# Columns whose layer-1 products are done at once: their transposed adjacency goes from SBUF into the weight table, not by way of DRAM

## The chip, the core and the metric

The kernel runs on one core of one Trainium2 chip. The metric is the device time of one execution in microseconds (us). Engines are named as the profile names them: PE multiplies matrices and transposes, DVE and ACT work on vectors, POOL issues the indirect gathers, SP issues plain DMAs; ACT issues some DMAs too. All DMAs run on the same sixteen DMA engines. A profile is one execution seen by the hardware profiler.

## What is computed

Two layers over a graph of 3,327 nodes (padded to 3,328 = 26 x 128) with 128 features and a sparse weighted adjacency matrix `adj`, symmetric in its pattern, about 2% full. Layer 0 is graph attention with four heads, layer 1 a normalised graph convolution:

```python
h = jnp.maximum(_layernorm(x, axis=-1), 0.0)
# for each of 4 heads
x1 = h @ w1
x2 = h @ w2
E = leaky_relu(x1[:, None, :] + x2[None, :, :], 0.01)
s = tanh(E @ a / 8.0) * 8.0
s = jnp.exp(s) * adj
s = s / jnp.sum(s, axis=-1, keepdims=True)
out = leaky_relu(s @ h @ Wlin.T, 0.01)
x = x + jnp.concatenate(heads, axis=-1) @ w

h = jnp.maximum(_layernorm(x, axis=-1), 0.0)
A_t = adj + jnp.eye(n)
D_inv = A_t.sum(axis=1) ** (-0.5)
A_norm = D_inv[:, None] * A_t * D_inv[None, :]
x = x + relu(A_norm @ (h @ W.T + b))
```

## The kernel before

Rows are handled in 26 blocks of 128. A row has few neighbours, so layer 0 does not form the full score matrix. `prep(b)` finds, for each row of block b, its neighbours' numbers; `gather` fetches one table row per neighbour with indirect DMAs (`DMA_INDIRECT`, L605, 128 table rows at a time, issued by POOL); the scores and the weighted sums are then made from what was fetched.

**The tables.** There are two tables in DRAM, `tables[0]` and `tables[1]`; block b uses `tables[b % 2]`. A table has one row of 776 numbers for each node: 64 numbers of adjacency (`FEAT`), 648 of features and products (`BODY`), 64 more of adjacency (`FEAT`). The 648 are written once, at the start. The adjacency numbers belong to a block: row n holds the weights `adj[r, n]` of block b's 128 rows r, the first 64 on one side of `BODY` and the other 64 on the other side, so that a gathered row brings its weights with it. They are the transposed 128 rows of `adj`, and are renewed for each block.

**How the weights get there.** `prep(b)` holds block b's rows of `adj` in SBUF (`adjb`, 128 x 3328, one buffer). `tables_step(j0)` (from L370) takes four column blocks (512 columns): PE transposes them into a PSUM bank (L373), ACT copies the bank to `at` in SBUF (L375; three buffers), and ACT issues a DMA that writes `at` to a scratch in DRAM, `AT_d` (L378). For 3,328 columns there are seven steps, the last of two column blocks. When all are done, `k.turned` is set, and `weights(b)` may be issued by SP: one DMA (L615) copies the whole 1,664 KB from `AT_d` into the table, DRAM to DRAM, in pieces of 512 bytes (the last 64 numbers of one row and the first 64 of the next lie side by side); a second, tiny one (L617) writes the first row's first 64 numbers.

**Who else reads `at` and `AT_d`.** Layer 1 needs the same transposed adjacency, times the finished features of the nodes in those columns. For columns whose features are already finished when block b is prepared, the product is made at once: `finished(b)` = max(0, 4 (b // 4) - 2) column blocks. `known_step` multiplies `at` with `x_sb` (PE, L387) and adds to `part1` (L391, L393), which goes to DRAM when complete (L395). The other columns are read back from `AT_d` late, at the end of layer 0 and in layer 1 (L929, L946).

**Order of the work.** All instructions are laid out in one order written by generators; each engine runs its own in that order. `prep` is a generator of up to 72 steps a block, advanced by `advance` in `slot()` alongside the groups of attention work of the block before; it runs about one to one and a half blocks ahead. Its course: steps of `codes` (L418) and of MAX8 on 64 segments (L430), with a `tables_step` at every eighth segment; then `turned`; then ACT's pass over `adjb` that sums the rows (`deg`, L451, 2.96 us), which is the last reader of `adjb`; then SP's load of the next block's rows into it (L359, 1,664 KB); then eight rounds of `select(r)` (L461, L464), the index lists, and the extras. POOL's gathers stand in a queue: 64 for the lists and 4 for the extras (`ge`) a block; `weights(b + 1)` stands in that queue behind the second group of gathers of block b, and is held until block b + 1 is turned. Gathered rows have four buffers `g` of eight gathers each; a buffer is free when PE has made the products `ag` (L680) from it.

**After layer 0's blocks** come the strips of layer 1 (L929 on), which read what is left from `AT_d`.

Of the kernel before, what the change touches and what calls it, by code (L numbers as in the profile page):

```python
# [10 lines left out]
AF = mybir.ActivationFunctionType  # L11
# [4 lines left out]
P = 128  # L16
# [48 lines left out]
FEAT = 64  # L65
BODY = 648
ROW = FEAT + BODY + FEAT
# [164 lines left out]
def _sparse_layers(tc, nc, x, adj, w1, w2, a, wlin, w, gw, gb, gb_sb, gwT, x_sb, dinv, flag, ident, out):  # L232
# [13 lines left out]
    NP, D = x.shape  # L246
    H = w1.shape[0]
    NB = NP // P
# [5 lines left out]
    NW = NT // WT  # L254
    LATE = 1

    with ExitStack() as l0:
        res = l0.enter_context(tc.tile_pool(name="res", bufs=1))
        dram = l0.enter_context(tc.tile_pool(name="dram", bufs=1, space=bass.MemoryType.DRAM))
        tables = [dram.tile([(NP + 1) * ROW], F32, name=f"table{k}") for k in range(2)]  # L260
# [3 lines left out]
        TURN = NP * P + HALF  # L264
        AT_d = dram.tile([NB * TURN], F32, name="AT_d")
# [87 lines left out]
        def finished(b):  # L353

            return max(0, 4 * (b // 4) - 2)

        def load(b):
            blks[b].adjb = pa.tile([P, NP], F32, name="adjb")
            nc.sync.dma_start(blks[b].adjb, adj[b * P:(b + 1) * P, :])  # L359

        def prep(b, k):
# [7 lines left out]
            def tables_step(j0):  # L369
                n = min(4, NB - j0)  # L370
                pt = ps_tr.tile([P, 4, P], F32, name="tr")
                for q in range(n):
                    nc.tensor.transpose(pt[:, q, :], adjb[:, (j0 + q) * P:(j0 + q + 1) * P], ident)  # L373
                at = pat.tile([P, 4, P], F32, name="at") if b else blks[0].at[j0 // 4 % 4]
                nc.scalar.copy(at[:, :n, :], pt[:, :n, :])  # L375
                at0 = b * TURN + j0 * P * P
                eng = nc.scalar if b else nc.sync
                eng.dma_start(AT_d[at0:at0 + n * P * P].rearrange("(p b c) -> p b c", p=P, c=P), at[:, :n, :])  # L378
                js = range(min(n, finished(b) - j0))
                if len(js):  # L380
                    known.append(known_step(j0, js, at))

            def known_step(j0, js, at):
                assert all(blks[j0 + q].closed for q in js)
                pq = bank()
                for q in js:
                    nc.tensor.matmul(pq[:, :P], x_sb[:, j0 + q, :], at[:, q, :], start=(q == 0), stop=(q == js[-1]))  # L387
                yield
                if j0 == 0:
# [4 lines left out]
                if j0 + len(js) == finished(b):  # L394
# [7 lines left out]

            SOME = 8 + 4 * 32
            cand = pb.tile([P, 2, SOME + 4 * 32], F32, name="cand", bufs=1)
            tab_at = 0
            while b == 0 and tab_at < NB:
                tables_step(tab_at)
                tab_at += 4
            k.turned = b == 0
            yield  # L410
            codes = None
# [1 line left out]
            for sgm in range(64):  # L413
# [20 lines left out]
                if sgm % 4 == 3:  # L434
                    yield
                    known_on()
                if sgm % 8 == 5 and tab_at < NB:
                    tables_step(tab_at)
                    tab_at += 4
            while tab_at < NB or known:  # L440
                known_on()
                if tab_at < NB:
                    tables_step(tab_at)
                    tab_at += 4
# [6 lines left out]
            nc.scalar.activation(adjb, adjb, AF.Copy, accum_out=deg)  # L451
            if 0 < b < NB - 1:
                load(b + 1)
            lists = pb.tile([P, 64 + 51], F32, name="lists")
            k.lists = lists
            flat = cand[:, :, :SOME]
# [1 line left out]
            def select(r):  # L458
                top = lists[:, 8 * r:8 * r + 8]
                of = cand[:, r % 2, :SOME] if r < 4 else flat  # L460
                nc.vector.max(top, of)  # L461
                yield
                if 8 * r + 8 < 2 * SLOTS + EXTRA:
                    nc.vector.match_replace(out=of, in_to_replace=top, in_values=of, imm_value=0.0)  # L464
                yield

            for r in range(SLOTS // 4):
                yield from select(r)

            lq = pb.tile([P, 4, 8, 16], F32, name="lq", bufs=1)  # L470
            nc.vector.tensor_tensor(lq, modsel.rearrange("p (q s) -> p q s", q=8)[:, None].to_broadcast([P, 4, 8, 16]),
# [113 lines left out]
        def gather(b, hb, w):  # L585
# [22 lines left out]
            queue.extend((k, hb, w, partial(one, t)) for t in range(n))  # L608
            k.g[hb, w] = g

        def weights(b):

            assert blks[b].turned
            tab, of = tables[b % 2], AT_d[b * TURN:(b + 1) * TURN]
            nc.sync.dma_start(tab[FEAT + BODY:FEAT + BODY + NP * ROW].rearrange("(p r c) -> p r c", p=P, c=ROW)[:, :, :2 * FEAT],  # L615
                              of[FEAT:].rearrange("(p r c) -> p r c", p=P, c=P))
            nc.sync.dma_start(tab[:FEAT].rearrange("(p c) -> p c", p=16), of[:FEAT].rearrange("(p c) -> p c", p=16))  # L617

# [207 lines left out]
        blks = []  # L826
        for b in range(NB):
            k = Blk()
            k.f0 = FEAT, 0
            k.g, k.wq, k.b, k.ready, k.turned, k.closed = {}, {}, b, False, False, False  # L830
            blks.append(k)
        GAP = 5
        WIDTH = WT + OVT
# [563 lines left out]
```

## Time and profile before

| | |
|---|---|
| median of 13 runs | 2501.8 us (2496.19 to 2508.04) |
| profiled execution | 2495.8 us, span of the core 2493.7 us |
| TensorE clock granted, mean | 0.981 |
| POOL: gathers | 1,664 + 104, 0.95 us each, 0.30 us between |
| DMA queues' share of 16 engines' span | POOL 71.9%, SP 17.6%, ACT 5.5% |
| writes `AT_d<-at`, issued by ACT | 150 of 256 KB, 25 of 128 KB |
| copies `table<-AT_d` (L615), issued by SP | 26 of 1,664 KB |
| loads `adjb<-in_adj_dram`, issued by SP | 26 of 1,664 KB |

How to read it: the queue `q0` is POOL's, `q1` SP's, `q10` ACT's. A row of the costliest groups has the line, the engine, the operation and what it writes and reads, the count, then the busy time and the mean of one in ns, and after the second bar the engine's idle time just before such instructions and what ended most of it. "issue" stands for time in which the engine waited for nothing that the profile shows. The chain is followed back from the last instruction, at each step to what released it. Idle time of an engine that is not the bottleneck costs nothing. Shares of busy time are averages; a PE that is busy is not a PE at its peak.

### The profile page before, as it was taken

Reading aid. Unit: us, or ns where it says so; the run is one execution under the profiler, and the core shown is the slowest. Engines: PE = TensorE matmul, PEld = TensorE weight load, DVE = VectorE, ACT = ScalarE, POOL = GpSimd, SP = SyncE. Lnnn points to the kernel's source line nnn. Section 1 sums busy time; section 2 is a strip of 40 time slices with the busy share of each in tenths; the row PEclk is TensorE's granted clock in tenths of the full one; section 3 lists DMA queues with packets and bytes.
Section 4 is the critical chain, followed back from the end, with each engine's and each line's share of the span. In section 5 each row is a group of like instructions: output and inputs, shape, how many; then the busy total and the mean of one; then the engine's idle time right before and its main releaser. Section 6 shows DMA issues by size and latency. Waiting matters only on the chain.

```text
span 2493.7 us, 51987 instructions
## 1 busy us (share of the span) xinstructions
PE 2232.0 (90%) x19254; PEld 1593.5 (64%) x19254; DVE 2073.8 (83%) x6426; ACT 642.7 (26%) x1555; POOL 1805.4 (72%) x1885
## 2 busy tenths in 40 slices
PE   6589888989988998998999999999999999999996
PEld 4466666666666666666666666666667667666653
DVE  7588988898888898889889888888988988896633
ACT  4122222223222222322222222232222222221110
POOL 3577777777777777777777777777777777777750
PEclk9699999999999999999999999999999999999998
DMA  9999999999999999999999999999999999999994
GB/s 316 376 325 326 353 330 318 348 349 313 332 359 332 322 347 345 315 332 360 310 328 354 334 316 349 350 314 333 357 318 320 357 339 320 342 337 335 367 333 154
DMA packets 315829, 826.93 MB, mean 332 GB/s; under 512 B 39032, under 2 KB 161809, under 8 KB 312241
## 3 DMA queue, kind: packets, MB, share of 16 engines
q0 software_dynamic: 145088, 629.53, 71.9%
q1 hardware_dynamic: 137328, 143.26, 17.6%
q10 hardware_dynamic: 33152, 50.74, 5.5%
q8 instruction: 155, 2.54, 0.4%
q14 instruction: 106, 0.86, 0.1%
HBM read 754.47 MB, written 113.22 MB: 348 GB/s over the span
## 4 chain that ended last, share of the span: by engine, by line
PE 39%; DVE 28%; DMA 15%; POOL 11%; issue 6%; ACT 0%; ACTq 0%; DVEq 0%; SPq 0%; POOLq 0%
PE z L632 14%; DVE r L648 14%; DMA g<-table,idx 13%; POOL g L605 10%; PE s L667 10%; DVE cand L430 3%; PE ag L680 2%; PE z L637 2%; DVE codes L418 2%; DVE cand L464 2%; DVE lists L461 1%; PE tr L387 1%; PE tr L957 1%; PE z L1021 1%; PE tr L373 1%
## 5 line engine op out<-in xcount | busy, mean ns | idle before, releaser
L605 POOL DMA_INDIRECT g<-table,idx x1664 | 1646.3, 989 | 557.5 <-issue 422.8
L648 DVE TENSOR_TENSOR r<-z,x1n 128x1024 f32<-128x1024 f32 x832 | 1010.8, 1215 | 134.6 <-PE z L632 132.4
L632 PE MATMUL z<-ident,g 128*128 128x128 f32 x6656 | 927.3, 279 | 121.1 <-DVE r L648 95.8
L632 PEld LDWEIGHTS z<-ident,g 128*128 128x128 f32 x6656 | 754.6, 143 | 259.2 <-DVE r L648 143.1
L667 PE MATMUL s<-r,sel 128*4 128x512 f32 (+1 forms) x3744 | 511.2, 581 | 12.5 <-DVE r L648 12.0
L708 ACT COPY ssb<-s 128x512 f32<-128x512 f32 x208 | 122.0, 587 | 516.7 <-PE s L667 516.7
L667 PEld LDWEIGHTS s<-r,sel 128*4 128x4 f32 x3744 | 85.4, 85 | 264.2 <-issue 186.3
L430 DVE MAX8 cand<-codes 128x8 f32<-128x52 uint16 x1664 | 217.5, 205 | 0.0
L680 PEld LDWEIGHTS ag<-g,wt 128*32 128x32 f32 x3328 | 116.9, 110 | 102.2 <-issue 95.2
L680 PE MATMUL ag<-g,wt 128*32 128x133 f32 x3328 | 159.5, 278 | 0.0
L740 ACT ACTIVATE sc<-sc 128x32 f32<-128x32 f32 x208 | 47.9, 230 | 407.7 <-DVE sc L735 257.3
L643 DVE TENSOR_TENSOR r<-z,x1n 128x128 f32<-128x128 f32 x104 | 30.1, 289 | 147.8 <-PE z L637 147.5
L375 ACT COPY at<-tr 128x512 f32<-128x512 f32 (+1 forms) x175 | 97.2, 556 | 211.3 <-PE tr L373 203.2
L461 DVE MAX8 lists<-cand 128x8 f32<-128x272 f32 (+1 forms) x338 | 133.2, 394 | 2.2
L645 ACT ACTIVATE r<-z 128x512 f32<-128x512 f32 x104 | 62.1, 597 | 256.7 <-DVE r L643 256.7
L605 POOL DMA_INDIRECT ge<-table,idxo x104 | 103.4, 994 | 31.8 <-issue 12.3
L719 PE MATMUL tr<-ident,ssb 128*128 128x128 f32 x832 | 125.4, 273 | 0.0
L373 PE MATMUL tr<-ident,adjb 128*128 128x128 f32 x676 | 108.2, 283 | 18.1 <-DMA adjb<-in_adj_dram 10.6
L637 PE MATMUL z<-oi,x1b 128*128 128x256 f32 x416 | 124.2, 380 | 0.0
L464 DVE MATCH_REPLACE8 cand<-lists,cand 128x272 f32<-128x272 f32 (+1 forms) x312 | 118.0, 378 | 0.0
L418 DVE SCALAR_TENSOR_TENSOR codes<-adjb,code 128x832 uint16<-128x832 f32 x104 | 104.1, 1017 | 12.2 <-DMA adjb<-in_adj_dram 12.2
L632 PE MATMUL z<-ident,ge 128*128 128x128 f32 x416 | 82.6, 280 | 26.6 <-DVE r L648 26.3
(209 smaller groups left out, 2467.2 us busy)
## 6 DMA issues: line engine op xcount, KB each, us to landing
adjb<-in_adj_dram SPq DMA_DIRECT2D x26, 1664.0 KB
table<-AT_d SPq DMA_DIRECT2D x26, 1664.0 KB
AT_d<-at ACTq DMA_DIRECT2D x150, 256.0 KB
g<-table,idx POOLq DMA_INDIRECT x1664
table<-img SPq DMA_DIRECT2D x12, 1296.0 KB
adjb<-AT_d SPq DMA_DIRECT2D x72, 128.0 KB
ge<-table SPq DMA_DIRECT2D x26, 178.0 KB
ge<-table SPq DMA_DIRECT2D x26, 177.2 KB
```

Source lines behind the costliest of these rows:

```text
L373: nc.tensor.transpose(pt[:, q, :], adjb[:, (j0 + q) * P:(j0 + q + 1) * P], ident)
L418: nc.vector.scalar_tensor_tensor(codes[:, i], adjb[:, c0:c0 + part], 0.0, code[:, c0:c0 + part], op0=OP.not_equal, op1=OP.mult, accum_out= ...
L430: nc.vector.max(cand[:, c, 8:].rearrange("p (r s) -> p r s", s=32)[:, :, sgm % 32], codes.rearrange("p a b -> p (a b)")[:, sgm % 32 * SEG: ...
L461: nc.vector.max(top, of)
L464: nc.vector.match_replace(out=of, in_to_replace=top, in_values=of, imm_value=0.0)
L605: return nc.gpsimd.indirect_dma_start(out=g[:, t, lo:hi], out_offset=None, in_=tab, in_offset=bass.IndirectOffsetOnAxis(ap=at[:, t:t + 1], ...
L632: nc.tensor.matmul(z[:, i, q * P:(q + 1) * P], g[:, m % 2 * 4 + q, c0:c0 + D], ident, is_transpose=True, start=(q == 0 or m < 8), stop=(m ...
L637: nc.tensor.matmul(z[:, i, :n], k.x1b[:, h * D:(h + 1) * D], k.oi[:, hb * n:(hb + 1) * n], start=False, stop=True, skip_group_check=True)
L648: nc.vector.tensor_tensor(r.rearrange("p h (i s) -> p h i s", s=16), z.rearrange("p h (i s) -> p h i s", s=16), k.x1n[:, 2 * hp:2 * hp + 2 ...
L667: nc.tensor.matmul(k.s[32 * h:32 * h + 4, :n], sel[:, h, 31 - row:35 - row], r[h // 2][:, h % 2, :n], start=(row == 0), stop=(last and (m ...
L680: nc.tensor.matmul(k.ag[32 * cg:32 * cg + 32, u, :WORK], wt[:, t].rearrange("p h q -> p (h q)"), g[:, t, f0:f0 + WORK], start=(w == 0 and ...
L719: nc.tensor.transpose(pt[:, q, :], ssb[:, q * P:(q + 1) * P], ident)
```

## The change

For a group of four column blocks all of which are finished, `tables_step` no longer writes `at` to `AT_d`. SP issues two DMAs that write it from SBUF straight into the table: one of three pieces of 512 bytes for each partition, one of two pieces of 256 bytes (the first 64 numbers of a partition's first row, the last 64 of its fourth). `weights(b)` copies only the rows that are left. A partition of `at` holds four neighbouring table rows.

The old content of `tables[b % 2]` serves block b - 2, so those steps come later in `prep`: the columns that still go through `AT_d` are turned first, alongside the segments, and the others one by one before the fourth and later rounds of `select`. ACT's pass over `adjb` and the load of the next block's rows, which overwrites `adjb`, move behind the last of them. There are no such steps in blocks 0 to 7, one each in blocks 8 to 11, two in 12 to 15, three in 16 to 19, four in 20 to 23 and five in 24 and 25. `part1` is complete when all finished columns are counted, in whatever order.

```diff
                 js = range(min(n, finished(b) - j0))
+                if len(js) == 4:
+                    assert table_is_free(b)
+                    rows = tables[b % 2][j0 * P * ROW:(j0 + 4) * P * ROW].rearrange("(p u) -> p u", p=P)
+                    flat = at.rearrange("p j c -> p (j c)")
+                    nc.sync.dma_start(rows[:, FEAT + BODY:FEAT + BODY + 3 * ROW].rearrange("p (r c) -> p r c", r=3)[:, :, :2 * FEAT],
+                                      flat[:, FEAT:FEAT + 3 * P].rearrange("p (r c) -> p r c", r=3))
+                    nc.sync.dma_start(bass.AP(rows.tensor, rows.offset, [list(rows.ap[0]), [3 * ROW + FEAT + BODY, 2], [1, FEAT]]),
+                                      bass.AP(flat.tensor, flat.offset, [list(flat.ap[0]), [4 * P - FEAT, 2], [1, FEAT]]))
+                else:
+                    at0 = b * TURN + j0 * P * P
+                    eng = nc.scalar if b else nc.sync
+                    eng.dma_start(AT_d[at0:at0 + n * P * P].rearrange("(p b c) -> p b c", p=P, c=P), at[:, :n, :])
...
-            tab_at = 0
+            whole = finished(b) // 4 * 4
+            turns, late = [*range(whole, NB, 4)], [*range(0, whole, 4)]
...
-            nc.scalar.activation(adjb, adjb, AF.Copy, accum_out=deg)
-            if 0 < b < NB - 1:
-                load(b + 1)
+
+            def last_readers():
+                nc.scalar.activation(adjb, adjb, AF.Copy, accum_out=deg)
+                if 0 < b < NB - 1:
+                    load(b + 1)
+
+            if not late:
+                last_readers()
...
             for r in range(SLOTS // 4):
+                if r >= 3 and late:
+                    tables_step(late.pop(0))
+                    if not late:
+                        last_readers()
                 yield from select(r)
+                known_on()
...
         def weights(b):
             assert blks[b].turned
-            tab, of = tables[b % 2], AT_d[b * TURN:(b + 1) * TURN]
+            row0 = finished(b) // 4 * 4 * P
+            tab, of = tables[b % 2][row0 * ROW:], AT_d[b * TURN + row0 * P:(b + 1) * TURN]
...
```

More of the change, by code (lines that the diff above doesn't have):

```diff
@@ L375, in tables_step @@
                 nc.scalar.copy(at[:, :n, :], pt[:, :n, :])
-                at0 = b * TURN + j0 * P * P
-                eng = nc.scalar if b else nc.sync
-                eng.dma_start(AT_d[at0:at0 + n * P * P].rearrange("(p b c) -> p b c", p=P, c=P), at[:, :n, :])
                 js = range(min(n, finished(b) - j0))
+                if len(js) == 4:
[10 more added lines that the diff above has]
+                    eng.dma_start(AT_d[at0:at0 + n * P * P].rearrange("(p b c) -> p b c", p=P, c=P), at[:, :n, :])
                 if len(js):
@@ L388, in known_step @@
                 yield
-                if j0 == 0:
+                if k.part1 is None:
                     k.part1 = pb.tile([P, P], F32, name="part1", bufs=1)
@@ L393, in known_step @@
                     nc.vector.tensor_add(k.part1, k.part1, pq[:, :P])
-                if j0 + len(js) == finished(b):
+                k.summed += len(js)
+                if k.summed == finished(b):
                     nc.sync.dma_start(part1_d[b // 4][:, b % 4 * P:(b % 4 + 1) * P], k.part1)
@@ L404, in prep @@
             cand = pb.tile([P, 2, SOME + 4 * 32], F32, name="cand", bufs=1)
-            tab_at = 0
-            while b == 0 and tab_at < NB:
-                tables_step(tab_at)
-                tab_at += 4
+            whole = finished(b) // 4 * 4
+            turns, late = [*range(whole, NB, 4)], [*range(0, whole, 4)]
+            while b == 0 and turns:
+                tables_step(turns.pop(0))
             k.turned = b == 0
@@ L436, in prep @@
                     known_on()
[L437 to L440, printed above, removed]
+                if sgm % 8 == 5 and turns:
+                    tables_step(turns.pop(0))
+            while turns or known:
                 known_on()
-                if tab_at < NB:
-                    tables_step(tab_at)
-                    tab_at += 4
+                if turns:
+                    tables_step(turns.pop(0))
                 yield
@@ L467, in prep @@
             for r in range(SLOTS // 4):
+                if r >= 3 and late:
+                    tables_step(late.pop(0))
+                    if not late:
+                        last_readers()
                 yield from select(r)
+                known_on()
+            while known:
+                known_on()
+            assert not late
             lq = pb.tile([P, 4, 8, 16], F32, name="lq", bufs=1)
@@ L609, in gather, with table_is_free @@
             k.g[hb, w] = g
+        def table_is_free(b):
+            before = (b - 1) * 2 * (NW + 1)
+            return state["fetched"] >= before + 2 and not any(q[0] is blks[b - 2] for q in queue)
         def weights(b):
             assert blks[b].turned
-            tab, of = tables[b % 2], AT_d[b * TURN:(b + 1) * TURN]
-            nc.sync.dma_start(tab[FEAT + BODY:FEAT + BODY + NP * ROW].rearrange("(p r c) -> p r c", p=P, c=ROW)[:, :, :2 * FEAT],
+            row0 = finished(b) // 4 * 4 * P
+            tab, of = tables[b % 2][row0 * ROW:], AT_d[b * TURN + row0 * P:(b + 1) * TURN]
+            nc.sync.dma_start(tab[FEAT + BODY:FEAT + BODY + (NP - row0) * ROW].rearrange("(p r c) -> p r c", p=P, c=ROW)[:, :, :2 * FEAT],
                               of[FEAT:].rearrange("(p r c) -> p r c", p=P, c=P))
@@ L830, in _sparse_layers @@
             k.g, k.wq, k.b, k.ready, k.turned, k.closed = {}, {}, b, False, False, False
+            k.part1, k.summed = None, 0
             blks.append(k)
```

## The prediction

> **What bounds the kernel now.** I read the page first, then the waits of POOL, then one block of about 88 us (block 17) in order of time on POOL, ACT, PE, DVE and SP, then the chain over the same block. In rows in order of time the first two numbers are start and duration in us; in rows of waits, total us, times and longest.
>
> ```profile
> span 2493.7 us, 51987 instructions
> PE 2232.0 (90%) x19254; PEld 1593.5 (64%) x19254; DVE 2073.8 (83%) x6426; ACT 642.7 (26%) x1555; POOL 1805.4 (72%) x1885
> q0 software_dynamic: 145088, 629.53, 71.9%
> q1 hardware_dynamic: 137328, 143.26, 17.6%
> q10 hardware_dynamic: 33152, 50.74, 5.5%
> L605 POOL DMA_INDIRECT g<-table,idx x1664 | 1646.3, 989 | 557.5 <-issue 422.8
> ...
> POOL g L605 <- DMA g<-table,idx: 30.2, 87, 1.3
> POOL g L605 <- PE ag L680: 6.2, 4, 2.1
> ...
> 1665.21 0.95 POOL L605 DMA_INDIRECT g<-table,idx  x1 [0.30 <-issue]
> 1676.94 0.96 POOL L605 DMA_INDIRECT ge<-table,idxo  x1 [0.30 <-PE ag L680]
> 1678.20 0.95 POOL L605 DMA_INDIRECT g<-table,idx  x1 [0.30 <-issue]
> ```
>
> The page tempts one to say "DMA": the three queues fill 71.9 + 17.6 + 5.5 = 95% of the sixteen engines. But look at POOL in order of time: a gather takes 0.95 us, the next begins 0.30 us later, whatever the releaser named, and so it goes across the border of a block (1676.94, 1678.20). A block has 68 gathers: 68 x 1.256 = 85.4 us. Block 17 ran from 1590.20 to 1678.20, 88.0 us; the other 2.5 us are gathers that took longer. Over the run such extra time sums to 65 us, 40 of it while DVE was at `codes` (L418) or `oi` (L520, L522): the gather at 1563.48 took 1.73 us, L418 began at 1563.37. In blocks 8 to 25, the only ones that change, the idle time between gathers above 0.303 us adds up to 4.4 us. POOL waits for a landing only 30.2 - 87 x 0.303 = 3.8 us in the whole run and for a buffer 6.2 - 4 x 0.303 = 5.0 us. So the writing of gather descriptors sets the pace, DMA has room of some 5%, and everything else matters only when it makes POOL wait.
>
> How near is that? A `g` buffer is free once PE's `ag` products have read it:
>
> ```profile
> 1663.00 0.66 PE L680 MATMUL ag<-g,wt 128*32 128x133 f32 x16
> ...
> 1590.19 2.96 ACT L451 ACTIVATE adjb<-adjb 128x3328 f32<-128x3328 f32 x1
> 1596.82 0.59 ACT L708 COPY ssb<-s 128x512 f32<-128x512 f32 x1 [3.58 <-PE s L667]
> 1604.88 0.60 ACT L645 ACTIVATE r<-z 128x512 f32<-128x512 f32 x1 [4.50 <-DVE r L643]
> 1607.66 0.60 ACT L645 ACTIVATE r<-z 128x512 f32<-128x512 f32 x1 [2.18 <-DVE r L643]
> ...
> 1607.55 0.43 DVE L461 MAX8 lists<-cand 128x8 f32<-128x272 f32 x1
> 1652.77 1.02 DVE L418 SCALAR_TENSOR_TENSOR codes<-adjb,code 128x832 uint16<-128x832 f32 x1
> ...
> 1593.27 0.33 SPq L359 DMA_DIRECT2D adjb<-in_adj_dram  x1
> 1594.43 0.50 SPq L615 DMA_DIRECT2D table<-AT_d  x1
> 1594.98 24.26 SPq L617 DMA_DIRECT2D table<-AT_d  x1
> 1620.75 0.46 SPq L597 DMA_DIRECT2D ge<-table  x1
> ...
> 1610.30 0.95 POOL g L605
> 1611.55 6.75 DMA g<-table,idx
> ```
>
> PE is done at 1663.66, POOL wants that buffer at 1665.21: 1.5 us of slack, the tightest of block 17. The same difference at each block's tightest buffer is 1.5 to 5.5 us in blocks 8 to 24. A delay below it costs nothing, the part above it costs in full.
>
> **The change, part by part.** The sum is made against the profiled execution, 2495.8 us (span 2493.7 and 2.1 around it); the median shown, 2501.8, is 6.0 above it, and I carry those 6.0 along. Of the 175 turning steps (`tables_step`), 50 become late ones: one each in blocks 8-11, two in 12-15, three in 16-19, four in 20-23, five in 24-25.
>
> Removed with each: an ACT issue (0.33 us) of a 256 KB write to `AT_d`, and the quarter MB of the DRAM copy L615 that read it back. In the trace's packet records the 2,048-byte packets of ACT's queue took 86.0 ns, the 512-byte ones of SP's 28.1: 128 x 86.0 + 512 x 28.1 = 25.4 us of one engine, 1.6 us of sixteen. Added: two SP writes, 384 pieces of 512 bytes and 256 of 256 bytes. No packet of 256 bytes is in the trace: between the 4-byte ones (9.8 ns) and two of 512 bytes (56 ns), I take one of 512, to which it is nearest: 640 x 28.1 = 18.0 us of one engine, 1.1 of sixteen (ends 13.3 and 25.2). Net -0.5 us of all engines a step, -23 us in all (ends -38 and 0). Cover: POOL's 1.256 us a gather; what it costs without cover is the second rival. On the path: 0.
>
> Here a rule speaks against the change. The Trainium skill, "DMA: Bandwidth & Descriptors", Specifications, wants pieces of at least 512 bytes, since smaller ones are read, modified and written back. Priced by it, my estimate is two full pieces for each half one, 56 ns, and the DMA gain is nil. No row here shows it.
>
> POOL's instructions: the same 1,768 gathers, 0. The first gather of a block has up to ten more writes to wait for, on at most eight semaphores; POOL's semaphore waits have a median of 43 ns and run while the gather before is at work (0.95 us): 0; uncovered, 18 x 8 x 0.043 = 6 us. Table 18 is complete in time: its last late write would be issued near 1606, the first gather from it is at 1678.20.
>
> SP: the order becomes hTb, the shorter L615, L617, the late writes, load of the next rows, part1, ge. L617 stood 24.26 us behind 3,328 pieces; now 2,816 down to 768 are ahead of it, and up to 3,200 pieces of late writes follow. A full queue holds ge (1620.75) a few us at worst, and POOL asks for that half's extras only at 1630.66. SP has 0.4 us more per write: idle time. The writes also wait for the turned copies and for the older gathers from that table, which W (L615) waited for already: 0.
>
> The load of the next rows moves from 1593.27 to after the last late step: with five of them, select 7 (1607.55) + about 3 us for transposes and copy + 3.15 us for L451, about 1614. Its packets ran from 1594.8 to 1602.2 and held the gathers' data packets down to 18 per us (some 53 to 57 otherwise). Behind five late steps (200 pieces an engine, at about 13 per us, the pace of L615's in the packet records, 15 us from 1601.5) it would run from about 1617 to 1625. Needed: 1652.77. Cover 27 us: 0. The gathers' 6.75 us to landing (1611.55) comes some 15 us later instead, not longer, because the three transfers only change places: 0.
>
> ACT and PE: transposes, copies and products keep their number and move 10 to 20 us later (the running sum `part1` now begins with the last two known columns: one ACT copy and the same DVE adds). L451's 2.96 us leave a hole of 3.58 us in which nobody waited and fall between 1601 and 1614, where m = 8's L645 stands. Bounds: 0, and 3 us a block. With four or five late steps the fourth copy also needs the first of three staging buffers back: issued near 1601.5, drained in 40/13 = 3 us, landed at most 3.54 us after that (a whole landing of a gather in the quiet part of the chain, at 1559.71), so by 1608, against a copy wanted at about 1606: 0 to 2 us, in which one of PE's two banks for transposes is held too. Both are delays of PE, not of POOL. PE stands idle 9% of the time here (busy 182.35 of the 200 us from 1500), 8 us a block, and the tight buffer comes 50 us later, so I take 0 on POOL; the upper end, 5 us less 1.5 slack in 14 blocks, is 49 us, not reached unless every delay adds up.
>
> Sum: 2495.8 + 0 + 6.0 = 2501.8; with the small end of the crowding, 0.2 us in a dozen blocks, 2504. I round to 2503.
>
> **Rivals.**
> *ACT is crowded (slower).* L451 and the waiting copies delay scores, `ag` frees `g` late, POOL waits. It decides above 1.5 to 5.5 us a block. For it: the hole that L451 loses, the slack. Against: PE's 9% idle. At 1 us a block in the 14 blocks with two or more late steps: 2516; at 2 us 2530.
> *DMA is the pace after all (faster).* For it: 95% busy, 11% of the chain in the block looked at is landings. Against: POOL's constant 0.30. It would give 2501.8 - 23 = 2479; if only the 4.4 us of idle goes, 2497.
> *DVE stretches gathers differently.* The 2.5 us a block depend on where L418 meets a gather (block periods range from 87.4 to 89.2): +-0.5 us in 18 blocks, 2493 to 2511.
> *The load comes too late.* If the queue held it past 1652.77, DVE would wait at L418. It needs 27 us more than I work out; 5 us in the six blocks with most late steps gives 2532.
>
> **How the numbers follow.** A difference below 0.2% (5 us) is about what cannot be told from no change here. Forecast, no change: 0.47. Crowded ACT: 0.25, all slower. DMA pace: 0.12, all faster. Stretches: 0.12, half each way beyond the bound (0.06 faster, 0.06 slower). Load late: 0.04, slower. So faster 0.18, same 0.47, slower 0.35. The range takes in the idle time won and the stretches below, 2490, and most of the crowding above, 2522; the far ends, 2479 and 2532, are left out with some 0.15. The forecast's own range is 2498 to 2506.
>
> **What would show it.** Right: L605 still 68 in about 88 us with 0.30 between them in blocks 8 to 25; ACT's writes to `AT_d` 125 instead of 175; q10's share near 4.1%; DVE's `codes` (L418 before) still without a wait for a load. ACT crowded: "POOL g <- PE ag" grows from 6 us to tens, ACT's copies `at` wait for a DMA in blocks 20 to 25. DMA pace: POOL's idle below 0.30, block periods under 87. Load late: DVE `codes` waits for the load of `adjb`. Most likely to prove me wrong is the slack of 1.5 us: many small delays that each pass it.

## The result, and the profile after

The changed kernel takes 2555.5 us (median of 8 runs, 2550.1 to 2558.5); the kernel before, with more runs beside it, 2502.5 (37 runs). The ratio is 1.0212, with a 95% interval of 1.0201 to 1.0224. The forecast was 2503 us and its range ended at 2522: the change is 2.1% slower, and the forecast was wrong.

The page of the profiled execution (2553.25 us) says that the change did what it says, and where the time is missing:

```profile
span 2551.5 us, 52051 instructions
PE 2265.4 (89%) x19254; PEld 1601.9 (63%) x19254; DVE 2076.1 (81%) x6426; ACT 641.4 (25%) x1555; POOL 1813.9 (71%) x1885
...
q0 software_dynamic: 145088, 629.53, 71.8%
q1 hardware_dynamic: 145328, 143.27, 17.4%
q10 hardware_dynamic: 25952, 37.63, 4.1%
...
L626 POOL DMA_INDIRECT g<-table,idx x1664 | 1658.3, 997 | 604.0 <-issue 425.6
```

ACT's queue fell from 5.5% to 4.1% of the sixteen engines, SP's from 17.6% to 17.4%. The number of matmuls is the same. POOL's `g` gathers show the loss: the idle time before them grew from 557.5 to 604.0 us (+46.5), their own time from 1646.3 to 1658.3 (+12.0). The gathers of the extras, with the idle time before them, took 3.7 us less, and 3.0 us came after the last gather: 46.5 + 12.0 - 3.7 + 3.0 = 57.8, which is the whole difference of the spans (2551.5 - 2493.7). So the whole loss can be read on POOL, which now waits. For what, its waits say (total us, times, longest):

```profile
POOL g L626 <- PE ag L707: 48.8, 16, 6.1
POOL g L626 <- DMA g<-table,idx: 31.6, 82, 2.3
```

and its order of time in block 22:

```profile
2097.05 0.95 POOL L626 DMA_INDIRECT g<-table,idx  x1 [0.30 <-issue]
2102.20 0.95 POOL L626 DMA_INDIRECT g<-table,idx  x1 [4.20 <-PE ag L707]
2103.46 0.95 POOL L626 DMA_INDIRECT g<-table,idx  x1 [0.30 <-issue]
```

The wait for a buffer that PE has not freed was 6.2 us in four places; it is 48.8 us in 16, and in blocks 19 to 24 it is one stop of 4.2 to 6.1 us a block. The wait for landings hardly changed (30.2 before). Summed over blocks with the same number of late steps in preparation, the gathers' periods grew by 1.3 us (blocks 7-10, one late step), 3.8 (11-14, two), 13.1 (15-18, three), 20.9 (19-22, four) and 13.2 (23 and 24, five): some 0.3, 1, 3.3, 5.2 and 6.6 us a block.

Why PE is late is seen when one block is cut into eight stages, from PE's first transpose of one buffer `g` (`z`, L632 before, L659 after) to that of the next. The windows of block 21, in whose last stages block 23 with its four late steps is in preparation, first of the kernel before (stages 1, 5, 6, 7, 8 and the sum; start and end, length, then the busy time of PE, PEld, DVE, ACT and POOL, the granted clock, DMA's share, GB/s):

```profile
1959.19:1965.57 6.38, 5.94 (x53) 4.87 (x51) 5.83 (x15) 1.67 (x4) 4.86 (x6) 1.00 1.05 404
...
2002.45:2011.90 9.45, 8.09 (x69) 6.82 (x68) 8.63 (x30) 3.10 (x7) 7.62 (x7) 1.00 0.89 280
2011.90:2024.63 12.73, 12.03 (x116) 9.91 (x115) 12.40 (x47) 3.81 (x9) 9.68 (x11) 1.00 0.98 321
2024.63:2033.82 9.19, 7.50 (x76) 5.34 (x74) 9.12 (x40) 3.91 (x6) 6.75 (x9) 1.00 1.01 370
2033.82:2047.19 13.37, 12.38 (x120) 8.32 (x121) 11.64 (x32) 2.70 (x6) 10.32 (x11) 1.00 1.00 373
sum 88.00, PE 81.37 PEld 59.99 DVE 78.13 ACT 23.89 POOL 67.28; mean PE 10.17 PEld 7.50 DVE 9.77 ACT 2.99 POOL 8.41
```

and the same stages after:

```profile
1997.26:2004.35 7.09, 6.44 (x55) 4.88 (x53) 5.76 (x15) 2.89 (x6) 5.53 (x6) 1.00 1.04 387
...
2041.18:2049.14 7.96, 6.64 (x57) 5.37 (x55) 7.18 (x23) 3.10 (x7) 6.43 (x6) 1.00 0.84 271
2049.14:2062.24 13.10, 9.98 (x85) 6.88 (x85) 12.86 (x49) 2.41 (x7) 10.05 (x11) 1.00 0.97 302
2062.24:2071.54 9.30, 7.28 (x69) 4.99 (x69) 9.23 (x42) 1.05 (x3) 7.17 (x8) 1.00 0.91 309
2071.54:2090.01 18.47, 17.66 (x168) 13.75 (x169) 12.81 (x37) 5.62 (x9) 13.90 (x16) 1.00 1.02 346
sum 92.75, PE 83.44 PEld 60.57 DVE 78.30 ACT 23.77 POOL 67.70; mean PE 10.43 PEld 7.57 DVE 9.79 ACT 2.97 POOL 8.46
```

Stages 5 to 7 lost 3.72 us of PE's work (27.62 to 23.90) and became 1.01 us shorter (31.37 to 30.36): in them DVE, with the segments' and selects' MAX8, is busy for nearly all of the time (12.86 of 13.10 us, 9.23 of 9.30), and it sets their length. Stage 8 got 5.28 us of PE's work and became 5.10 us longer: there PE was busy 12.38 of 13.37 us already. Stage 1, in which ACT's pass over `adjb` now lies, is 0.71 longer. PE's work keeps its number of instructions, but it went from where DVE sets the pace to where PE does.

The chain, followed back over the same place, goes through that work (start, length, what, how many):

```profile
2086.24 1.09 PE tr L396 x8
2087.32 0.45 PE tr L373 x4
2087.80 0.58 ACT at L375
2088.38 2.97 ACT adjb L461 x2
2091.35 0.49 ACT r L672
2091.89 0.71 PE s L694 x4
```

L373 are the transposes of a late step (0.44 us of PE by the starts of what follows), L396 its layer-1 products (0.89 to 1.0); 4 x (0.44 + 0.89) = 5.3 us, as much as the 5.28 of stage 8. Behind the fourth step ACT makes the last copy and then the pass of 2.97 us, and the relu `r` (L672), for which the scores (L694) wait, stands behind both.

### The profile page after: what moved, and what is told of

Same layout as the page of the kernel before. It is cut to its first block, busy times and chain, and to the rows that moved or that the text cites. A ratio compares the mean times of both kernels' runs of the same rounds, so it can differ in the third digit from the quotient of the medians.

```text
span 2551.5 us, 52051 instructions
## 1 busy us (share of the span) xinstructions
PE 2265.4 (89%) x19254; PEld 1601.9 (63%) x19254; DVE 2076.1 (81%) x6426; ACT 641.4 (25%) x1555; POOL 1813.9 (71%) x1885
## 3 DMA queue, kind: packets, MB, share of 16 engines
q1 hardware_dynamic: 145328, 143.27, 17.4%
## 4 chain that ended last, share of the span: by engine, by line
PE 36%; DVE 27%; DMA 15%; POOL 14%; issue 7%; ACT 1%; SPq 0%; ACTq 0%; DVEq 0%; POOLq 0%
DVE r L675 13%; POOL g L626 13%; DMA g<-table,idx 12%; PE z L659 12%; PE s L694 9%; DVE cand L440 4%; PE ag L707 2%; PE z L1049 2%; PE z L664 2%; DVE codes L428 2%; PE tr L985 1%; DVE lists L474 1%; DVE cand L477 1%; DVE wo L718 1%; PE z L1167 1%
## 5 line engine op out<-in xcount | busy, mean ns | idle before, releaser
L626 POOL DMA_INDIRECT g<-table,idx x1664 | 1658.3, 997 | 604.0 <-issue 425.6
L659 PE MATMUL z<-ident,g 128*128 128x128 f32 x6656 | 922.3, 279 | 142.7 <-DVE r L675 115.9
L659 PEld LDWEIGHTS z<-ident,g 128*128 128x128 f32 x6656 | 751.2, 142 | 284.9 <-DVE r L675 165.5
L694 PE MATMUL s<-r,sel 128*4 128x512 f32 (+1 forms) x3744 | 543.1, 593 | 23.5 <-DVE r L675 21.5
L694 PEld LDWEIGHTS s<-r,sel 128*4 128x4 f32 x3744 | 86.1, 86 | 302.8 <-issue 192.2
L707 PEld LDWEIGHTS ag<-g,wt 128*32 128x32 f32 x3328 | 124.8, 111 | 101.1 <-issue 93.3
L670 DVE TENSOR_TENSOR r<-z,x1n 128x128 f32<-128x128 f32 x104 | 30.2, 290 | 184.5 <-PE z L664 184.3
L707 PE MATMUL ag<-g,wt 128*32 128x133 f32 x3328 | 173.8, 280 | 0.0
L767 ACT ACTIVATE sc<-sc 128x32 f32<-128x32 f32 x208 | 47.8, 230 | 393.1 <-DVE sc L762 241.3
L373 PE MATMUL tr<-ident,adjb 128*128 128x128 f32 x676 | 107.2, 281 | 26.1 <-DMA adjb<-in_adj_dram 11.0
L428 DVE SCALAR_TENSOR_TENSOR codes<-adjb,code 128x832 uint16<-128x832 f32 x104 | 104.1, 1017 | 12.7 <-DMA adjb<-in_adj_dram 12.7
L672 ACT ACTIVATE r<-z 128x512 f32<-128x512 f32 x104 | 62.0, 596 | 190.3 <-DVE r L670 190.0
L373 PEld LDWEIGHTS tr<-ident,adjb 128*128 128x128 f32 x676 | 81.1, 145 | 31.0 <-issue 12.4
```

The costliest lines, as they stand in the source:

```text
L428: nc.vector.scalar_tensor_tensor(codes[:, i], adjb[:, c0:c0 + part], 0.0, code[:, c0:c0 + part], op0=OP.not_equal, op1=OP.mult, accum_out= ...
L626: return nc.gpsimd.indirect_dma_start(out=g[:, t, lo:hi], out_offset=None, in_=tab, in_offset=bass.IndirectOffsetOnAxis(ap=at[:, t:t + 1], ...
L659: nc.tensor.matmul(z[:, i, q * P:(q + 1) * P], g[:, m % 2 * 4 + q, c0:c0 + D], ident, is_transpose=True, start=(q == 0 or m < 8), stop=(m ...
L694: nc.tensor.matmul(k.s[32 * h:32 * h + 4, :n], sel[:, h, 31 - row:35 - row], r[h // 2][:, h % 2, :n], start=(row == 0), stop=(last and (m ...
L707: nc.tensor.matmul(k.ag[32 * cg:32 * cg + 32, u, :WORK], wt[:, t].rearrange("p h q -> p (h q)"), g[:, t, f0:f0 + WORK], start=(w == 0 and ...
```

## Experiments

The theories, as the expectations number them. Theory 1: the moved pass of ACT delays the scores. Theory 2: the moved turning work costs, 2a by its time on PE, 2b by its banks, copies and staging buffers. Theory 3: the route itself, the late load or SP's queue cost. Ratios are to the kernel before on the same chip, with 95% intervals.

### The route alone

A third table lets the turning steps stay at their old place: block b from 8 on takes `tables[b % 3]`, whose old content served block b - 3. SP writes finished columns from SBUF as in the change; turning, pass and load keep their old order.

```diff
-        tables = [dram.tile([(NP + 1) * ROW], F32, name=f"table{k}") for k in range(2)]
+        tables = [dram.tile([(NP + 1) * ROW], F32, name=f"table{k}") for k in range(3)]
...
+        def turn_of(b):
+            return b % 2 if b < 8 else b % 3
...
-            turns, late = [*range(whole, NB, 4)], [*range(0, whole, 4)]
+            turns, late = [*range(0, NB, 4)], []
...
```

> The route alone. A third table (filled DRAM to DRAM with the fixed part during blocks 1 to 7) serves blocks 8, 11, 14 and on, so that a block's table is free when its columns are turned; all turning steps, the pass and the load stand where they stood before the change, and the finished columns are written from SBUF straight into the table by SP as in the change. Theories 1 and 2: 0.997 to 1.004, with blocks 8 to 24 at 87.5 to 89 us. Theory 3 (pieces of 256 bytes, SP's queue, staging buffers): 1.01 or more, blocks from 16 on at 90 us or more. If DMA traffic were worth something: under 0.997.

Measured: 2503.8 us, ratio 1.0006 (0.9995 to 1.0017). From its page:

```profile
q1 hardware_dynamic: 148768, 151.90, 18.6%
q10 hardware_dynamic: 25952, 37.63, 4.2%
...
L636 POOL DMA_INDIRECT g<-table,idx x1664 | 1645.3, 989 | 565.4 <-issue 413.4
```

and from POOL's waits:

```profile
POOL g L636 <- PE ag L717: 3.3, 4, 1.6
```

The same 50 + 50 writes by SP, the same fall of ACT's queue, and nothing lost or won (q1 has six copies of 1,296 KB and one of 648 KB more, which fill the third table in blocks 1 to 7). The route with its third table costs nothing, so theory 3's share can only be in the late load; the loss comes from the order that two tables force. It also speaks against the rival on DMA: from block 8 on, ACT's and SP's packets take 31 us of all sixteen engines less by the packet records, and the kernel is not faster. The gathers' own packets took 23 us longer in the same stretch, so the three queues together still fill 95% of the engines: that share tells little of the room that DMA has.

### The third table without the route

The control for it: the kernel before with a third table and nothing else.

> The kernel before with a third table and nothing else: blocks from 8 on take the tables by threes, the way through the scratch in DRAM stays. The route alone, with the third table, gave 1.0006. If the third table is free, 0.998 to 1.002 here, and the route itself is free. If the third table costs (1.003 or more), the route gains what the third table costs; if the third table alone is faster (0.997 or less), the route costs that much.

> As e9_third_table, on a chip where the kernel before takes 2500 us: 0.998 to 1.002 if the third table is free and so is the route; 1.003 or more if the third table costs what the route gains; 0.997 or less if the route costs.

Measured: 1.0009 (0.9982 to 1.0035) and 0.9998 (0.9967 to 1.0029). In both, the kernel before takes 3340 to 3530 us, with PE's granted clock at 0.87 to 0.89 (called a chip of low clock below); several of the experiments below were first run so too. The lower clock is not the whole reason: in the profile of the first run with the late load, PE is busy 2515 us of 3350 (75%; the kernel before on the usual chip has 2232 of 2494, 90%), and it stands idle for 406 us in gaps of over 3 us (30 us in that kernel). What makes these gaps is not known. POOL waits for PE in most of its buffers there:

```profile
POOL g L608 <- PE ag L683: 872.1, 172, 13.0
```

so what hides behind PE there can't be seen. On a chip of the usual clock the control wasn't run: whether the third table hides a small gain or loss of the route is not shown.

### The pass back

The changed kernel with ACT's pass ahead of the selects again; the late steps and the load stay late.

```diff
+            nc.scalar.activation(adjb, adjb, AF.Copy, accum_out=deg)
+
             def last_readers():
-                nc.scalar.activation(adjb, adjb, AF.Copy, accum_out=deg)
                 if 0 < b < NB - 1:
```

> The changed kernel, but ACT's pass over the rows (2.96 us, L461 there) goes back to its old place ahead of the selects; late turning steps and the load of the next rows stay late. In the changed kernel the pass stands on the chain in block 22 (2088.38, 2.97 us) with ACT's relu of the extras behind it (2091.35). Theory 1, the moved pass: most of the 53 us goes, ratio to the kernel before 1.000 to 1.006, the gap of 4 to 6 us a block in which POOL waits for PE's ag goes to under 2 us. Theory 2, the moved turning work of PE and ACT: ratio stays at 1.015 to 1.021, gap 4 us or more. Theory 3, the moved load or the writes on SP's queue: ratio stays at 1.02.

Measured: 2549.6 us, ratio 1.0194 (1.0177 to 1.0211) against 1.0212. Stages 1, 7 and 8 of block 21:

```profile
1996.13:2002.32 6.19, 5.75 (x55) 4.81 (x53) 5.65 (x15) 1.30 (x4) 4.77 (x5) 1.00 1.02 371
...
2060.21:2070.27 10.06, 8.44 (x69) 5.08 (x69) 9.35 (x42) 2.90 (x4) 7.62 (x9) 0.83 0.91 294
2070.27:2088.75 18.48, 17.66 (x168) 13.76 (x169) 12.81 (x37) 5.46 (x11) 13.91 (x16) 1.00 1.02 344
```

Stage 1 gets its 0.9 us back, stage 7 gives 0.76 of it away in a stretch of lower clock, stage 8 is as long as with the pass behind it. POOL's waits for PE's `ag` are 41.9 us in 19 places, against 48.8 in 16. Theory 1 is not the main cause.

### Pass and load late, nothing else

The kernel before, with its pass and its load moved to where the change has them.

```diff
...
+            if not steps:
+                last_readers()
...
             for r in range(SLOTS // 4):
+                if steps and r == 2 + steps:
+                    last_readers()
                 yield from select(r)
```

> The kernel before, with only ACT's pass over the rows and the load of the next rows moved to where the change has them (ahead of select 3 in blocks 8 to 11, 4 in 12 to 15, up to 7 in 24 and 25); turning steps and route as before. Theory 1 (the pass): 1.012 to 1.02. Theory 2 (the turning work): 0.999 to 1.005. Theory 3 in the form that the late load crowds out gathers: 1.012 to 1.02 too, but then the chain there runs over landings of gathers and not over ACT.

Measured: 2519.6 us, ratio 1.0058 (1.0041 to 1.0075); stage 1 of block 21 is 7.05 us instead of 6.38. That lies between the ranges expected for theories 1 and 2. Moved without the turning steps, pass and load together make 0.58% of the change's 2.12%, about a quarter. Which of the two it is was to be told by the load moved alone:

> The kernel before with only the load of the next rows issued late (ahead of the same selects as with the pass and the load late, which gave 1.0058); ACT's pass stays in its old place. If the pass behind ACT's other work made the 1.0058: 0.998 to 1.002. If the late load's large packets made it, crowding out gathers: 1.004 to 1.007.

> The kernel before with only the load of the next rows moved to the place it has in the change; the pass of ACT stays ahead of the selects, every turning step at its old place. With pass and load moved the ratio was 1.0058. If the pass made those 0.6%: 0.998 to 1.002 here. If the load's large packets, coming later, made them: 1.004 to 1.007, with longer gathers (above 0.95 us) around the new place of the load.

> As e8_again, on a chip where the kernel before takes 2500 us: if the pass made the 0.6% of the moved pass and load, 0.998 to 1.002; if the load, 1.004 to 1.007.

Measured: 1.0009 (0.9982 to 1.0036), 1.0011 (0.9990 to 1.0032), 1.0018 (0.9986 to 1.0049), all three on chips of low clock, where POOL waits for PE in most buffers anyway. The load alone can't be told from nothing there; on the usual chip it stays open.

### The late order with the old route

The changed kernel's order, but each late `at` goes to `AT_d` first (ACT's queue), and SP's two writes read it from there.

```diff
-                    flat = at.rearrange("p j c -> p (j c)")
+                    at0 = b * TURN + j0 * P * P
+                    flat = AT_d[at0:at0 + n * P * P].rearrange("(p c) -> p c", p=P)
+                    nc.scalar.dma_start(flat.rearrange("p (b c) -> p b c", c=P), at[:, :n, :])
```

> The changed kernel's order with the old route: a late step's ACT copy is written to the scratch in DRAM, and SP's two writes, of the same shapes as in the change, read it from there. Theories 1 and 2 (the order costs): ratio 1.018 to 1.025. Theory 3 in the form that the writes out of SBUF (three staging buffers held by SP's queue) cost: at most 1.008.

Measured: 2564.6 us, ratio 1.0250 (1.0233 to 1.0267). The late order costs by the old route too, and somewhat more. In ACT's order of time the pass now waits for the write of its last copy, and stage 1 of block 21 is 8.58 us:

```profile
2091.81 0.58 ACT L375 COPY at<-tr 128x512 f32<-128x512 f32 x1 [2.89 <-PE tr L373]
...
2093.59 2.98 ACT L463 ACTIVATE adjb<-adjb 128x3328 f32<-128x3328 f32 x1 [1.20 <-DMA AT_d<-at]
```

With the route alone at 1.0006, this is the cleanest pair: the order is the cause, the route is not.

### The changed kernel without the late products

The layer-1 products of the late steps are left out, and with them that part of layer 1's sum; the transposes, copies and writes stay.

```diff
-                if len(js):
+                if len(js) == 4:
+                    k.summed += 4
+                elif len(js):
                     known.append(known_step(j0, js, at))
...
```

> The changed kernel without the layer-1 products of the late steps (their part of the sum is left out; per late step four products on PE, about 1.1 us of the step's 1.55 us of PE, and one add on DVE). Theory 2a, PE has no room in the select stretch and the moved PE time itself is what costs: 50 x 0.44 us of transposes and the moved pass are left, most of it inside the slack, ratio 1.003 to 1.010, POOL's wait for PE's ag in blocks 19 to 23 under 2 us. Theory 2b, not PE's time but the turning itself (transposes held up by two PSUM banks, ACT's copies, SP's queue): 1.014 or more.

> The changed kernel without the layer-1 products of the late steps, once more, on a chip where the kernel before takes about 2500 us (the first time it took 3339 us with a granted clock of 0.89 and PE held POOL up throughout, so that run says little about a kernel in which POOL sets the pace). Theory 2a (PE's moved time): 1.003 to 1.010, POOL's wait for PE's ag in blocks 19 to 23 under 2 us a block. Theory 2b (turning itself, banks, copies, SP): 1.014 or more.

Measured: 0.9753 (0.9715 to 0.9791) on a chip of low clock; on the usual one 2542.4 us, ratio 1.0166 (1.0131 to 1.0201). The total lies where theory 2b was expected, not 2a, and POOL's waits for PE's `ag`, 47.7 us, are hardly less than in the changed kernel. But the sums by blocks say more than the total. The periods of blocks 15-18 and of 23 and 24 grew by only 5.3 and 6.3 us over the kernel before, against 13.1 and 13.2 with the products; stage 8 of block 17 (three late steps) is 13.37 us against 17.14 with them, and 13.4 before the change. So the products in stage 8 are more than half of the loss in these blocks. But in blocks 19-22 the loss rose from 20.9 to 31.4. What came there, in order of time on ACT:

```profile
1886.09 0.60 ACT L674 ACTIVATE r<-z 128x512 f32<-128x512 f32 x1 [2.55 <-DVE r L672]
1891.76 0.59 ACT L375 COPY at<-tr 128x512 f32<-128x512 f32 x1 [5.07 <-DMA table<-at]
1892.24 2.98 ACT L463 ACTIVATE adjb<-adjb 128x3328 f32<-128x3328 f32 x1
...
1895.21 0.59 ACT L674 ACTIVATE r<-z 128x512 f32<-128x512 f32 x1
```

and on PE:

```profile
1888.78 1.04 PE L661 MATMUL z<-ident,g 128*128 128x128 f32 x8
...
1895.86 1.24 PE L696 MATMUL s<-r,sel 128*4 128x320 f32 x4 [5.40 <-ACT r L674]
1897.02 1.97 PE L661 MATMUL z<-ident,g 128*128 128x128 f32 x8
```

Without the products the steps follow each other faster, and the fourth copy waits 5.07 us for the first of the three staging buffers, until SP's write of it has landed. The pass and the relu stand behind it, PE waits 5.40 us, and then eight transposes take 1.97 us instead of 1.04, at a lower clock. In blocks 19-22 the clock stood at half for 51.2 us in all, against 10.2 us in the changed kernel, so how the 31.4 us divide between the staging buffers and the clock is not settled. Both halves of theory 2 have a part: 2a is the larger in blocks 15-18, 23 and 24 and, by the stages of block 21, in the changed kernel as it is; 2b comes out when 2a is taken away.

### PE work added to the kernel before

Nothing is moved; as many times as the block has late steps, four transposes and four products are made into a PSUM bank that nobody reads, ahead of the select rounds from the fourth on (first) or beside the segments (second).

```diff
+            def extra_step():
+                pq = bank()
+                for q in range(4):
+                    nc.tensor.transpose(pq[:, q * P:(q + 1) * P], x_sb[:, q, :], ident)
+                for q in range(4):
+                    nc.tensor.matmul(pq[:, :P], x_sb[:, q, :], ident, start=(q == 0), stop=(q == 3))
...
+                if 3 <= r < 3 + extras:
+                    extra_step()
```

The second has, in place of the last two lines, in the loop over the segments:

```diff
+                if sgm % 8 == 1 and sgm // 8 < extras:
+                    extra_step()
```

> The kernel before plus PE work alone (four transposes and four products into a PSUM bank that nobody reads, about 1.5 us of PE), once ahead of each select from 3 on, as often as the change has late steps; nothing moved, same route. Theory 2a: added PE time in the select stretch reaches POOL once the slack of 1.5 to 5 us is gone: 1.010 to 1.022. Theory 2b: at most 1.004.

> The kernel before plus about 1.5 us of PE work ahead of each select from 3 on, as often as the change has late steps, once more where the kernel before takes about 2500 us. Theory 2a: 1.010 to 1.022. Theory 2b: at most 1.004.

> The same added PE work, as often, but in the stretch of codes and MAX8 where DVE is busiest, beside the old turning steps. Theory 2a says that PE has room there, since it waits for DVE: at most half of what the run with the work in the select stretch loses, 1.000 to 1.008. If any added PE time costs wherever it stands, both lose the same.

> The same added PE work among the segments, once more where the kernel before takes about 2500 us. Theory 2a with room in that stretch: 1.000 to 1.008 and at most half the loss of the run with the work in the selects. If added PE time costs wherever it stands (where the kernel before took 3339 us it cost 1.029 here and 1.0125 in the selects, against the theory): 1.010 or more here too, and then the changed kernel's loss needs another reason than the stretch, since it adds no PE work.

Measured beside the selects: 1.0125 (1.0090 to 1.0161) on the chip of low clock, 1.0136 (1.0116 to 1.0155) on the usual one; beside the segments 1.0288 (1.0257 to 1.0319) and 1.0162 (1.0142 to 1.0183). Stage 8 of block 21 in the first, stages 5 and 6 in the second:

```profile
2056.73:2073.99 17.26, 17.26 (x168) 13.60 (x169) 11.83 (x32) 2.69 (x6) 13.29 (x14) 1.00 1.00 377
```

```profile
2031.76:2044.35 12.59, 12.11 (x106) 10.81 (x105) 11.70 (x40) 3.10 (x7) 9.85 (x10) 1.00 0.88 276
2044.35:2058.39 14.04, 13.34 (x128) 11.23 (x127) 9.64 (x37) 3.80 (x9) 9.60 (x10) 1.00 0.92 286
```

One such step is 1.33 us of PE by the starts of its rows, four are 5.3. In the first kernel the block grew by 3.88 us (88.00 to 91.88), all of it in stage 8; in the second by 4.48, in stages 5 and 6. This corrected the theory: the segments' stretch has no room for PE work either. In the kernel before it was balanced (stage 5: PE 8.09, DVE 8.63 of 9.45 us; stage 6: 12.03 and 12.40 of 12.73). Taking PE work out of it gains little because DVE holds it, putting some in costs because PE does. Block 21 as a whole has room for 5.3 less 3.9 to 4.5, about 1 us of PE work. Earlier blocks have more: with two such steps a block (2.7 us) the periods of blocks 11-14 grew by -0.1 us in the first kernel and 1.4 in the second, in the sum of the four.

### Less PE work in the kernel before

If PE alone were the bound, taking work from it would pay. In the kernel before, the early layer-1 products are left out for all finished columns but the last two, and with them that part of layer 1's sum: eight products for each of the 50 steps.

```diff
-                if len(js):
+                if len(js) and j0 + len(js) == finished(b):
                     known.append(known_step(j0, js, at))
...
```

> The kernel before without the early layer-1 products of all finished columns but the last two: up to some 18 x 0.056 us of PE work and its share of the sums leave each late block, so a part of layer 1's sum is left out. If POOL and PE are both at their limit here (theory of the pace kept by both): 0.997 to 1.001, POOL's period stays near 87 to 88 us and the slack at the tightest buffer grows above 4.2 us. If PE alone were the bound and POOL only followed: 0.985 or less.

> As e10_few_products, on a chip where the kernel before takes 2500 us. Both at their limit: 0.997 to 1.001, with the slack at the tightest buffer above 4.2 us. PE alone the bound: 0.985 or less, with POOL's period below 87 us.

> As e10_again, on a chip where the kernel before takes 2500 us. Both POOL and PE at their limit: 0.997 to 1.001, POOL's period near 87 to 88 us, slack at the tightest buffer above 4.2 us. PE alone the bound there: 0.985 or less, with POOL's period below 87 us.

Measured: on two chips of low clock 0.9873 (0.9843 to 0.9903) and 0.9843 (0.9785 to 0.9901); on the usual one 2509.6 us, ratio 1.0020 (1.0008 to 1.0032), just above the range expected for both at their limit (the profiled run is the slowest of its ten, 2517.5 us). The sums of four windows from 1500 to 2300 us, first of the kernel before, then of this one:

```profile
sum 800.00, PE 740.60 PEld 542.19 DVE 698.47 ACT 211.52 POOL 609.61; mean PE 185.15 PEld 135.55 DVE 174.62 ACT 52.88 POOL 152.40
```

```profile
sum 800.00, PE 715.13 PEld 508.49 DVE 688.47 ACT 210.16 POOL 605.46; mean PE 178.78 PEld 127.12 DVE 172.12 ACT 52.54 POOL 151.36
```

PE is relieved of 25 us in 800, and POOL goes no faster. PE caught up with the gathers: in these 800 us its transposes `z` wait for gathered rows 21 times, 11.5 us in all, and not once in the kernel before. So in the kernel before POOL's gathers do set the pace on a chip of the usual clock, as the prediction said; with its full work PE never catches up with them, and by the runs with added work its late blocks can take little more. The slack at the tightest buffer, which I expected to stay above 4.2 us, was 4.2 to 6.1 in blocks 17, 19, 20, 21 and 22 (1.5 to 4.0 before), but 3.7 and 1.7 in blocks 18 and 23: there the expectation failed. Why the kernel is even 0.2% slower is open; its granted clock is lower (0.974 over the span against 0.981).

## Why the prediction was wrong

**The bound.** Right: POOL's gathers, 0.95 + 0.30 us, set the pace of the kernel before; the run with fewer products shows it. What was missed is that PE, right behind, had next to no room. That "PE ag" grew "from 6 us to tens" was named as the sign of crowding, and it came: 48.8.

**DMA.** Right: the two queues' work fell and nothing came of it (the rival at 2479 us fell with the route alone at 1.0006). The writes to `AT_d` are 125 and q10's share 4.1%, as said. The price of the piece of 256 bytes was too high: 12,800 of them took 18.4 ns each in the trace's packet records, where I had taken 28.1. The Trainium skill, "DMA: Bandwidth & Descriptors", Specifications, has pieces below 512 bytes read, modified and written back; an estimate of two full pieces made 56 ns of that, and this case's packets disagree with that estimate: a piece of 256 bytes cost less than one of 512 (29.6 ns after the change).

**POOL's waits for semaphores, the late writes, the load.** Taken at nothing, and no wait speaks against it; only whether the late load makes gathers longer stayed open. `codes` (L428) waits for a load once in the whole run, 12.7 us, as before (once, 12.2). SP's order is the one worked out, here for table 23 with four late steps:

```profile
2071.49 0.50 SPq L642 DMA_DIRECT2D table<-AT_d  x1
2072.04 1.89 SPq L644 DMA_DIRECT2D table<-AT_d  x1
2077.51 0.38 SPq L381 DMA_DIRECT2D table<-at  x1
...
2088.81 0.49 SPq L383 DMA_DIRECT2D table<-at  x1
2091.38 0.34 SPq L359 DMA_DIRECT2D adjb<-in_adj_dram  x1
```

L644 stands 1.89 us, where L617 stood 24.26 for the prediction's block; the load comes 19.9 us after L642, where I had some 20.

**The staging buffer.** Bounded at 0 to 2 us; in the changed kernel copies waited for `table<-at` once, 3.6 us, above the bound but in one place only. It was that small because the products kept the steps apart: without them the waits are 21.0 us in four places.

**ACT's pass.** Bounded at 0 and 3 us a block. It measured about 0.7 us in stage 1 of block 21; undone, it brought the ratio from 1.0212 to 1.0194, intervals that overlap.

**The step that failed** is "transposes, copies and products keep their number and move 10 to 20 us later", with "PE stands idle 9% of the time here ..., 8 us a block, ... so I take 0 on POOL". The move itself was costed at nothing, and an average was read as room. By stages PE's idle 6.6 us of block 21 are 0.4, 1.0, 0.4, 0, 1.4, 0.7, 1.7 and 1.0 us, and none of them holds the 5.3 us of four late steps. Moved from stages 5 to 7, where DVE's MAX8 fix the length, to stage 8, the same instructions cost 5.1 us and gave 1.0 back. A sign of it stood in the trace of before: the slack at the tightest buffer was 1.5 us in blocks 17 and 18, 4.0 in 20 and 21, 2.4 in 23. It drifted, and did not build up. With 8 us a block to spare, PE would have caught up with POOL's gathers until it waited for data; from 1500 to 2300 us it did not once, and PE work added to a late block cost most of its length. The upper end of 49 us, "not reached unless every delay adds up", was passed: 57.8 us of span.

**The rivals.** "ACT is crowded" had the right sign, the right place at which POOL waits and a price near it (2530 us at 2 us a block; it was 3 to 7 in the late blocks), but the wrong engine: the largest part is PE's own moved work. How the rest of a late block's loss divides among the pass, the load, the staging buffer and stretches of lower clock was not settled; the clock can account for part of it only, since by its records PE had half clock for 47.8 us between 500 and 2250 us, 27.3 more than before, which I estimate at 13.7 us of its work at most. The rivals on DVE's stretches and on the late load (a wait at `codes`) did not come, except that the `g` gathers became 12.0 us longer in sum, more than the 9 us that I allowed to either side; where POOL waits for PE anyway, a longer gather shortens that wait, so whether they add to the loss is not shown. (The block periods of 87.4 to 89.2 us named with that rival are those of blocks 8 to 23; the last two took 86.3 and 85.8.)

## What to carry to other kernels

Idle time of an engine is no room unless one stage holds it in one piece: cut the loop into stages, write down the busy time of each engine in each, and price a moved step by the stage that it enters, crediting the stage that it leaves only down to its next fullest engine. A "free" reordering of equal work between a stage held by DVE and one held by PE cost 2%, while the transfer that it was for cost nothing. Whether a pipeline has room is told by its slack: if it doesn't grow from block to block, and the follower never waits for the leader's data, the follower is as slow as the leader.

## What was unexpected of the hardware

PE's clock stood at half more often where PE had less work, or where the same work was moved. By the trace's clock records (500 to 2250 us), the kernel before has six stretches of 3.4 us at half clock, the changed one twelve, of 3.4 or 6.8 us, and the one without the late products eighteen, of up to 13.7 us; the two with extra PE work have four and three. (The route alone, with the same work in its old place, has nine, so the count varies by itself too.) A window of the kernel without late products, around the wait of 5.40 us, holds one of these stretches, with PE busy 4.60 of 10 us and the granted clock at 0.66:

```profile
1890.00:1900.00 10.00, 4.60 (x23) 3.08 (x20) 3.00 (x5) 4.62 (x5) 7.56 (x9) 0.66 1.05 384
```

The Trainium skill, "TensorE: Matmul & The Clock Gate", Part 1, tells of windows of some 3.4 us and half rate after an idle one; the lengths here (one, two or four times 3.4 us) agree with it, but the windows ahead of the stretches were not idle. All stretches begin on one grid of 3.413 us. Of the windows of that grid at full clock in these five profiles, all 27 in which PE was busy for less than 47% were followed by half clock, 16 of the 141 with 47 to 66%, and none of the 2,345 with more. So here it is the busy share of a window that goes with the lower clock, and it takes no gap as long as the window (the longest ahead of a stretch was 3.36 us, most were under 1.7).

In block 21 of the changed kernel every stage has the clock at 1.00, so the loss does not need these stretches.

And where a kernel runs matters for what bounds it: the same removal of products is worth 1.3 to 1.6% in runs with a granted clock of 0.87 to 0.89, where POOL waits for PE more than 800 us, and nothing at 0.98. Whether it is the chip is open: the record has the kernel before at 2503 us and, less than an hour later, at 3343 us under the same chip number (8).
